# Six-bit weights read as float16 bit patterns, byte-paired words, and a rearranged start, in a fused conditioning and feed-forward kernel

## Chip, cores and metric

The kernel runs on one core of one Trainium2 chip. The metric is device time in microseconds (us). The time before is the median of three runs, 272.76 us (272.31 to 272.89).

## What is computed

The reference, cut to what matters:

```python
x: (64, 64, 1024) float32; itok: (64,) int32; weights: (16, 64, 64) float32
qweight: (1024, 768) int32; scale, zero_point: (1024, 1); bias: (1024,)
W = weights[itok]
h = einsum('bct,bcd->bdt', x, W)
p = qweight.reshape(1024, 256, 3)
v0, v1 = p[:, :, 0] & 63, p[:, :, 0] >> 6 & 63
v2, v3 = p[:, :, 1] & 63, p[:, :, 2] & 63
w = (stack([v0, v1, v2, v3], axis=2).reshape(1024, 1024) - zero_point) * scale
out = x + einsum('bsk,nk->bsn', h, w) + bias
```

Each of the 64 batches picks one of 16 small matrices, multiplies its 64 x 1024 block of x by it, and then multiplies the result by one shared 1024 x 1024 matrix of six-bit integers, with a zero point and a scale for each output feature.

## The kernel before

Batches go in pairs: 32 pairs, each 128 partitions (2 x 64 channels) by 1024 features, and two pairs make a group that shares one tile of x. The features are laid out by field, so that each 128-row tile of the weights (KT = 8 tiles) is one field of the packed words: tiles 0 and 1 are v0, 2 and 3 are v1, 4 and 5 are v2, 6 and 7 are v3.

Float32 factors are replaced by two float16 parts, a rounded high part and the remainder as a low part, so that TensorE can work in 16 bits. A pair goes through two products:

- The **first product** (`stage1`, L437) multiplies x by the selected conditioning matrix. Before it, a power of two for each batch is found from a sum of magnitudes (`magnitudes` on ScalarE L257, `bounds` on TensorE L261, `scales` on VectorE with `powers` L129 to L133). `split_1` (ScalarE, L281) writes the scaled high part, `split_2` (VectorE, L291) the low part, and four transfers on SyncE's queue (`stack_high` L303 and L304, `stack_low` L308 and L309) stack the parts in the tile `xa`. The conditioning table `tab` is split into parts in the same manner once (`weights_scaled` L189, `weights_high` L192, `weights_low` L195), and each pair's matrices are copied from it by two transfers (`select_pair`, L233).
- The **second product** (L461) multiplies the first one's result, again split into `hh` (ScalarE, L449) and `hl` (VectorE, L453), by the integer weights `qT`: 8 tiles x 2 parts x 2 banks of 512 columns, 32 products for each pair.
- VectorE then scales the sums by the batch's and the feature's scales (L502) and adds x (L507). ScalarE and GpSimd add the zero point's part (`zero_points` L495 and L497, which needs the feature sums, L326) and the bias (`add_bias`, L490) to x in place beforehand. Even pairs accumulate in one PSUM tile and odd pairs in another, so a pair's second product waits until the result of the pair two before has been read.

The order of instructions on every engine is written out by hand. A steady loop, `window(p)` from pair 3 on, issues the first product of pair p+1, the results of pair p-1, the splitting of a later group and then the second product of pair p.

Pairs 0 and 1 (group 0) have a start of their own, so that TensorE has real work early. Fifty products of a dummy (WARM, L520) come first. Their first products are done in float32 straight from x and the selected matrices (`early_stage1`, L383). Their scales come from a bound: the largest magnitude of x in each partition (`early_largest`, VectorE, L363) times the largest magnitude in each row of the selected matrix, which GpSimd copies from a table (`early_select`, L351 and L354); `early_rows` (L367) forms the product, `early_bounds` (TensorE, L371) sums it over the partitions, and `early_scales` turns it into powers of two. `early_high` (ScalarE, L391) and `early_low` (VectorE, L398) split the result. Pairs 0 to 3 have their results kept aside by `early_out` (L417, L421), which adds the zero point's part, and GpSimd adds these to x later (`early_add`, L426) in the windows named by `LATE` (L660).

In the same stretch the packed words arrive as six blocks of 16-bit halves (`load_q`, L76), VectorE masks or shifts out the six bits (`unpack`, L144 and L146), and a second instruction on VectorE or ScalarE (`centre`, L152 and L154) converts the integers to float16 less 32 (QMID). The zero points are turned into 32 less themselves (L600). The scale of the conditioning table is found by a float32 product with the identity (`weights_turn`, L170) and another that spreads the diagonal (`weights_bounds`, L182).

SyncE issues nearly all transfers, in program order.

Of the kernel before, what the change touches and what calls it, by code (L numbers as in the profile page):

```python
# [18 lines left out]
QMID = 32.0  # L19
# [9 lines left out]
def adaln_ffn(ctx: ExitStack, tc: tile.TileContext, x, cond, cw, qw, ws, wz, bias, out):  # L29
# [9 lines left out]
    WARM = 50  # L39
# [20 lines left out]
    def load_pair(p):  # L60
        g, i = divmod(p, 2)
        if i == 0:
            xts[g] = xp.tile([P, 2, T], F32, name="xt")
        nc.sync.dma_start(xts[g][:, i, :], xf[:, p, :])
# [6 lines left out]
    NW = qw.shape[1] // P  # L71
    qr = qp.tile([P, NW, N], U16, name="qr", bufs=1)
    qv = qw.rearrange("h (w p) n -> h p w n", p=P)

    def load_q(w, n=1):
        nc.sync.dma_start(qr[:, w : w + n, :], qv[0, :, w : w + n, :])  # L76
# [9 lines left out]
    load_pair(0)  # L86
    load_q(0)
    load_q(1)
    load_pair(1)
    load_q(2, 2)  # L90
    load_q(4, 2)
# [24 lines left out]
    spread = const.tile([NK, P], F32, name="spread")  # L116
# [7 lines left out]
    eye = const.tile([P, P], F32, name="eye")  # L124
    nc.vector.tensor_scalar(eye, off, 0, None, ALU.is_equal)

    def powers(sums, up, down):

        nc.vector.tensor_scalar(sums, sums, LEAST, None, ALU.max)  # L129
        nc.vector.tensor_scalar(  # L130
            down.bitcast(I32), sums.bitcast(I32), EXPONENT, EXPONENT, ALU.bitwise_and, ALU.bitwise_xor
        )
        nc.vector.tensor_scalar(up.bitcast(I32), sums.bitcast(I32), EXPONENT, None, ALU.bitwise_and)  # L133


    qT = const.tile([P, KT, N], F16, name="qT")
    qis = {}

    def unpack(kt, n=1):

        qi = qp.tile([P, n, N], U16, name="qi", tag=f"qi{n}")
        w = kt if kt < 2 else kt - 2
        if kt in (2, 3):
            nc.vector.tensor_scalar(qi, qr[:, w : w + n, :], 6, 63, ALU.logical_shift_right, ALU.bitwise_and)  # L144
        else:
            nc.vector.tensor_scalar(qi, qr[:, w : w + n, :], 63, None, ALU.bitwise_and)  # L146
        for m in range(n):
            qis[kt + m] = qi[:, m, :]

    def centre(kt, eng):  # L150
        if eng is nc.scalar:
            nc.scalar.activation(qT[:, kt, :], qis[kt], AF.Copy, bias=-QMID)  # L152
        else:
            eng.tensor_scalar(qT[:, kt, :], qis[kt], 1.0, -QMID, ALU.mult, ALU.add)  # L154
# [7 lines left out]
    wmx = const.tile([P, NK], F32, name="wmx")  # L162
# [10 lines left out]
    def weights_diagonal():  # L173
        most = const.tile([NK, 1], F32, name="most")
        nc.vector.tensor_reduce(most, tmp["pt"], AX.X, ALU.max)
        diag = const.tile([NK, NK], F32, name="diag")
# [20 lines left out]
    def weights_hot():  # L197

        hot = const.tile([NK, B], F32, name="hot")
# [5 lines left out]
        up_w = const.tile([NK, P], F32, name="up_w")  # L205
# [61 lines left out]
    def unscales(g):  # L267
        nc.vector.scalar_tensor_tensor(st[g]["u"], st[g]["up"], 0.25, wupb[:, 2 * g : 2 * g + 2], ALU.mult, ALU.mult)

    def scales_in_full(g):  # L270

        pl = st[g]["pl"]
        powers(pl, pl, st[g]["down"])
        nc.vector.scalar_tensor_tensor(st[g]["u"], pl, 0.25, wupb[:, 2 * g : 2 * g + 2], ALU.mult, ALU.mult)
# [36 lines left out]
    def split_sums(g):  # L311
        xs = st[g]["xs"]
        xh = sp.tile([P, 2, 2], F16, name="xh")
        for j, (h, o) in enumerate(((LO, HI), (HI, LO))):
            nc.scalar.copy(xh[h, :, j], xs[h, :])  # L315
            for i in range(2):
# [18 lines left out]
    def unscale_sums(g):  # L335
        for j, h in enumerate((LO, HI)):
            nc.vector.tensor_tensor(st[g]["hs"][h, :], st[g]["pu"][h, :, j], st[g]["u"][h, :], ALU.mult)  # L337


    xm = const.tile([P, 2], F32, name="xm")  # L340
    wm = const.tile([P, 2], F32, name="wm")
    pb = const.tile([P, 2, 2], BF, name="pb")
    updown = const.tile([P, 2, 2, 2], F32, name="updown")

    def early_select():

        for p in range(2):
            ks = []
            for j, h in enumerate((LO, HI)):
                k = nc.gpsimd.value_load(cb[0:1, 2 * p + j : 2 * p + j + 1], min_val=0, max_val=NK - 1)  # L350
                nc.gpsimd.tensor_copy(wbd[h, p, h], w32[h, ds(k, 1), :].rearrange("p o d -> p (o d)"))  # L351
                ks.append((h, k))
            for h, k in ks:
                nc.gpsimd.tensor_copy(wm[h, p : p + 1], wmx[h, ds(k, 1)])  # L354

    def early_sums(p):
        if 0 not in st:
            st[0] = {n: const.tile([P, 2], F32, name=n + "0") for n in ("xs", "u", "hs")}
# [3 lines left out]
    def early_largest(p):  # L362
        nc.vector.tensor_reduce(xm[:, p : p + 1], xts[0][:, p, :], AX.X, ALU.max, apply_absolute_value=True)  # L363

    def early_rows(p):

        nc.vector.tensor_scalar(pb[:, p, :], half, xm[:, p : p + 1], wm[:, p : p + 1], ALU.mult, ALU.mult)  # L367

    def early_bounds(p):
        pl = ps_s.tile([P, 2], F32, name="pl", tag="s")  # L370
        nc.tensor.matmul(pl, lhsT=all_ones, rhs=pb[:, p, :], start=True, stop=True)  # L371
        tmp["pl"] = pl

    def early_scales(p):
        powers(tmp["pl"], updown[:, p, 0, :], updown[:, p, 1, :])

    def early_unscales(p):
        for j, h in enumerate((LO, HI)):
            nc.vector.tensor_scalar(st[0]["u"][h, p : p + 1], updown[h, p, 0, j : j + 1], 0.5, None, ALU.mult)

    def early_stage1(p, ph, kts=range(KT)):
        for n, kt in enumerate(kts):
            nc.tensor.matmul(  # L383
                ph[:, n, :, :], lhsT=xts[0][:, p, ts(kt, P)], rhs=wbd[:, p, :], start=True, stop=True
# [29 lines left out]
    def early_out(p):  # L414
# [3 lines left out]
            pos[p], pos[p], st[g]["u"][:, i : i + 1], tmp["zt", p], ALU.mult, ALU.add  # L418
# [57 lines left out]
    def stage2_bank(p, n, ks=range(2)):  # L476
        if p not in pos:
            pos[p] = ps_o[p % 2].tile([P, N], F32, name="po", tag="po")
        for k in ks:
            products(pos[p], p, range(KT), [k], [BANKS[n]], [BANKS[n]])  # L480
# [11 lines left out]
    def zero_points(p):  # L492
# [4 lines left out]
        nc.gpsimd.tensor_tensor(xt, xt, zt, ALU.add)  # L497
# [28 lines left out]
    weights_largest()  # L526
    early_select()
    for n in range(2, 6):
        conditions_of(n)
    early_sums(0)  # L530
    early_largest(0)
    early_rows(0)
    early_stage1(0, ph0a, range(0, 4))
    early_bounds(0)
    unpack(0)
    early_scales(0)
    early_high(0, ph0a, LOWER)
    early_stage1(0, ph0b, range(4, KT))
    centre(0, nc.vector)
    unpack(1)  # L540
    centre(1, nc.vector)
    early_high(0, ph0b, UPPER)
    early_sums(1)
    stage2_tiles(0, range(0, 2), [0])
    early_low(0, ph0a, LOWER)
    early_stage1(1, ph1)
    unpack(2, 2)
    centre(2, nc.scalar)
    centre(3, nc.scalar)
    stage2_tiles(0, range(0, 2), [1])  # L550
    weights_turn()
    stage2_tiles(0, range(2, 3))
    early_largest(1)
    early_rows(1)
    unpack(4, 2)
    centre(4, nc.vector)
    early_bounds(1)
    stage2_tiles(0, range(3, 4))
    magnitudes(1, 0)
    centre(5, nc.scalar)  # L560
    early_low(0, ph0b, UPPER)
    early_scales(1)
    weights_diagonal()
# [3 lines left out]
    centre(6, nc.vector)  # L567
    early_high(1, ph1, slice(0, KT))
    stage2_tiles(0, range(5, 6))
    weights_bounds()  # L570
    scales(1, FIRST)
    centre(7, nc.vector)
    split_1(1, 0)
    stack_high(1, FIRST)
    load_x(3)
    magnitudes(1, 1)
    weights_powers()
    stage2_tiles(0, range(6, KT))
# [4 lines left out]
    bounds(1, SECOND)  # L583
    scales(1, SECOND)
    split_1(1, 1)
    weights_scaled()
    weights_high()
# [5 lines left out]
    select_pair(2)  # L593


    stage2_tiles(1, range(0, 4), [0])
    early_feature_sums(0)
    early_unscales(0)
    early_unscales(1)
    nc.scalar.activation(zsb, zsb, AF.Copy, bias=QMID, scale=-1.0)  # L600
    early_zero_points(0)
    stage2_tiles(1, range(0, 4), [1])
    stack_high(1, SECOND)
    split_2(1, 1)
    stack_low(1, SECOND)
    select_pair(3)
    nc.sync.dma_start(bib, bias.partition_broadcast(P))
    select_pair(4)
    select_pair(5)
    weights_hot()  # L610
    early_out(0)
    stage2_tiles(1, range(4, 7))
    magnitudes(2, 0)
    split_sums(1)
    ph = stage1(2)
    stage1_high(2, ph)
    magnitudes(2, 1)
    stage2_tiles(1, range(7, KT))
    early_feature_sums(1)
    early_zero_points(1)  # L620
# [3 lines left out]
    stage2_bank(2, 0, [0])  # L624
# [162 lines left out]
```

## Time and profile before

| | |
|---|---|
| median of three runs | 272.76 us |
| profiled execution | 272.38 us |
| its span, first to last instruction | 270.6 us |
| mean granted TensorE clock | 0.998 |
| TensorE products busy | 263.2 us (97% of the span) |
| VectorE busy | 204.8 us (76%) |
| ScalarE busy | 162.3 us (60%) |
| GpSimd busy | 168.2 us (62%) |
| second products (L461), hh and hl | 496 each of 512 columns, mean 379 ns |
| chain that ended last | TensorE 83% (L461 alone 70%), VectorE 10%, transfers 4% |

Times in the profile count from the start of the span. PE is TensorE, PEld its load of the stationary factor, DVE VectorE, ACT ScalarE, POOL GpSimd, SP SyncE; a q behind an engine's name means its queue of transfers. A group is written as output<-inputs, shapes, the number of instructions, its busy time, the mean of one in ns, and the idle time before it with what ended that. Products are pipelined, so a mean of 379 ns is a product's latency: the stream passes 32 of them in 6.91 us. The chain of waits is followed back from the last instruction, at each step to what released it.

Landings of the first loads, worked out from the issue times and times to landing: conditioning matrices 4.43 us, x of pair 0 5.82, the first two blocks of words 6.99 and 7.73, x of pair 1 9.01, the other words 10.4 and 11.7, x of pair 2 13.0 and of pair 3 15.3.

### The profile page before, as it was taken

To read this page: it belongs to the slowest core of one execution; us is meant where nothing else is said; L and a number is where in the kernel's file an instruction comes from. 1 tells how busy PE (TensorE), PEld (TensorE's weight loads), DVE (VectorE), ACT (ScalarE), POOL (GpSimd) and SP (SyncE) were. 2 spreads that over 40 slices of the span, in tenths; PEclk is the share of its full clock that TensorE was granted. 3 is DMA by queue.
4 is the path that set the end of the run, shared out by engine and by line. 5 is a ranking of instruction groups with operands and counts; after the bars stand their busy time and mean duration, and the time that the engine had idled before them with its cause. 6 is when DMAs were issued, how large, how long until landed. Compare 5 with 4: busy or idle time off the path is not lost.

```text
span 270.6 us, 5751 instructions
## 1 busy us (share of the span) xinstructions
PE 263.2 (97%) x2170; PEld 142.2 (53%) x2170; DVE 204.8 (76%) x272; ACT 162.3 (60%) x289; POOL 168.2 (62%) x87
## 2 busy tenths in 40 slices
PE   8999989999999999999999999999999999999994
PEld 8645545455555545555554555555455555545553
DVE  3989799795695959869595985959599595955543
ACT  3788897576565667656566765656676565634100
POOL 4100069969789595978959593874919387495200
PEclk9999999999999999999999999999999999999999
DMA  7997666975878796686965897696776765551203
GB/s 238 403 333 239 150 147 184 202 241 127 285 207 247 247 265 220 146 303 183 285 198 156 256 251 237 183 291 173 206 227 167 213 181 148 166 157 78 79 18 139
DMA packets 35836, 55.30 MB, mean 204 GB/s; under 512 B 18400, under 2 KB 18656, under 8 KB 35808
## 3 DMA queue, kind: packets, MB, share of 16 engines
q1 hardware_dynamic: 35776, 54.93, 68.1%
q8 instruction: 17, 0.28, 0.4%
q14 instruction: 11, 0.09, 0.1%
q10 hardware_dynamic: 32, 0.00, 0.0%
HBM read 20.45 MB, written 16.78 MB: 138 GB/s over the span
## 4 chain that ended last, share of the span: by engine, by line
PE 83%; DVE 10%; DMA 4%; ACT 1%; issue 1%; SPq 0%; DVEq 0%; ACTq 0%
PE po L461 70%; PE ph L437 9%; DVE lf L291 3%; PE pe L461 3%; DMA xa<-lf 2%; DMA xt<-in_x_dram 2%; DVE po L417 1%; DVE res L421 1%; DMA wst<-tab 1%; DVE hl L453 1%; PE ph L383 1%; PE pu L326 0%; ACT hf L281 0%; DVE xm L363 0%; DVE tab L195 0%
## 5 line engine op out<-in xcount | busy, mean ns | idle before, releaser
L461 PE MATMUL po<-qT,hh 128*128 128x512 f16 x496 | 118.5, 379 | 0.7 <-ACT hh L391 0.4
L461 PE MATMUL po<-qT,hl 128*128 128x512 f16 x496 | 118.5, 379 | 0.0
L497 POOL TENSOR_TENSOR xt<-xt,zt 128x1024 f32<-128x1024 f32 x28 | 79.3, 2852 | 51.4 <-ACT zt L495 51.4
L490 POOL TENSOR_TENSOR xt<-xt,bib 128x1024 f32<-128x1024 f32 x32 | 76.5, 2412 | 28.0 <-DVE hs L337 25.4
L461 PEld LDWEIGHTS <-hl 128*128 128x128 f16 x520 | 50.8, 98 | 59.1
L449 ACT CAST hh<-ph 128x1024 f16<-128x1024 f32 x30 | 30.3, 1011 | 80.9 <-PE ph L437 42.5
L461 PEld LDWEIGHTS <-hh 128*128 128x128 f16 x520 | 48.2, 98 | 52.7 <-ACT hh L391 0.6
L502 DVE SCALAR_TENSOR_TENSOR po<-po,u,scb 128x1024 f32<-128x1024 f32 x27 | 34.8, 1287 | 50.6 <-PE po L461 50.6
L291 DVE SCALAR_TENSOR_TENSOR lf<-xt,down,hf 128x1024 f16<-128x1024 f32 x30 | 62.4, 2118 | 0.7 <-ACT hf L281 0.7
L437 PEld LDWEIGHTS <-xa 128*128 128x128 f16 x960 | 32.3, 98 | 9.1 <-issue 1.5
L453 DVE TENSOR_TENSOR hl<-ph,hh 128x1024 f16<-128x1024 f32 x30 | 36.5, 1216 | 0.0
L281 ACT ACTIVATE hf<-xt,down 128x1024 f16<-128x1024 f32 x30 | 34.2, 1144 | 2.4 <-DVE down L130 2.2
L437 PE MATMUL ph<-wst,xa 128*128 128x64 f16 x960 | 33.3, 193 | 1.7 <-DMA xa<-lf 0.8
L507 DVE TENSOR_TENSOR xt<-po,xt 128x1024 f32<-128x1024 f32 x27 | 33.1, 1225 | 2.2 <-DVE po L502 0.5
L257 ACT ACTIVATE junk<-xt 128x1024 bf16<-128x1024 f32 x30 | 31.7, 1056 | 1.0 <-DMA xt<-in_x_dram 0.3
L495 ACT ACTIVATE zt<-zsc,hs 128x1024 f32<-128x1024 f32 x28 | 30.5, 1137 | 0.0
L318 ACT ACTIVATE xh<-xh,xs 64x1 f16<-64x1 f16 x60 | 14.4, 287 | 1.0
L426 POOL TENSOR_TENSOR xt<-xt,res 128x1024 f32<-128x1024 f32 x4 | 9.4, 2359 | 0.0
L461 PE MATMUL pe<-qT,hh 128*128 128x256 f16 (+1 forms) x24 | 6.6, 308 | 0.0
L520 PE MATMUL pc<-dummy 128*128 128x128 bf16 x50 | 5.5, 311 | 1.1 <-DVE one L102 1.1
L461 PE MATMUL pe<-qT,hl 128*128 128x256 f16 (+1 forms) x24 | 6.5, 308 | 0.0
L315 ACT CAST xh<-xs 64x2 f16<-64x2 f32 x30 | 5.7, 191 | 0.2
(82 smaller groups left out, 108.4 us busy)
## 6 DMA issues: line engine op xcount, KB each, us to landing
out_dram<-xt SPq DMA_DIRECT2D x31, 512.0 KB, 3.0
xt<-in_x_dram SPq DMA_DIRECT2D x14, 1024.0 KB, 7.6
xa<-hf SPq DMA_DIRECT2D x26, 256.0 KB, 3.8
xa<-lf SPq DMA_DIRECT2D x26, 256.0 KB, 3.8
xt<-in_x_dram SPq DMA_DIRECT2D x4, 512.0 KB, 7.6
wst<-tab SPq DMA_DIRECT2D x60, 32.0 KB, 3.0
qr<-in_L_ffn_qweight_dram SPq DMA_DIRECT2D x2, 512.0 KB, 7.6
xa<-hf SPq DMA_DIRECT2D x8, 128.0 KB, 3.0
```

The lines of the kernel that those rows point to most:

```text
L257: nc.scalar.activation(junk, xts[g][:, i, :], AF.Abs, accum_out=st[g]["l1"][:, i : i + 1])
L281: nc.scalar.activation(st[g]["hf"][:, i, ts_], xts[g][:, i, ts_], AF.Copy, scale=st[g]["down"][:, i : i + 1], accum_out=st[g]["xs"][:, i : ...
L291: nc.vector.scalar_tensor_tensor(st[g]["lf"][:, i, ts_], xts[g][:, i, ts_], st[g]["down"][:, i : i + 1], st[g]["hf"][:, i, ts_], ALU.mult, ...
L437: nc.tensor.matmul(ph[:, kt, j, :], lhsT=st[g]["xa"][:, i, j, ts(kt, P)], rhs=wsts[g][:, i, a, j, :], start=(a == 0), stop=(a == 1),)
L449: nc.scalar.copy(hs_pair[p][0][:, kts, :], ph[:, kts, :])
L453: nc.vector.tensor_tensor(hl[:, kts, :], ph[:, kts, :], hh[:, kts, :], ALU.subtract)
L461: nc.tensor.matmul(po[:, a], lhsT=hs_pair[p][k][:, kt, :], rhs=qT[:, kt, c], start=(kt == 0 and k == 0), stop=(kt == KT - 1 and k == 1),)
L490: nc.gpsimd.tensor_tensor(xt, xt, bib, ALU.add)
L495: nc.scalar.activation(zt, zsc, AF.Copy, scale=st[g]["hs"][:, i : i + 1])
L497: nc.gpsimd.tensor_tensor(xt, xt, zt, ALU.add)
L502: nc.vector.scalar_tensor_tensor(po, po, st[g]["u"][:, i : i + 1], scb[:, cols], ALU.mult, ALU.mult)
L507: nc.vector.tensor_tensor(xts[g][:, i, cols], po, xts[g][:, i, cols], ALU.add)
```

## The change

- **Weights.** The unpacked six bits are written straight into the tile that the second products read; its 16-bit words are taken as float16 bit patterns, so that an integer v stands for v x 2^-24 (QUNIT). `centre`, its tile and the pass over the zero points go. The factor 2^-24 is put into the scales (`0.25 / QUNIT`, `0.5 / QUNIT`, `unscale_sums`), and the zero point's part is subtracted instead of added.
- **Packed words.** The host's layout puts the six-bit bytes in pairs: four blocks instead of six; tiles 2 and 3 are blocks 0 and 1 shifted by 6, tiles 6 and 7 are blocks 2 and 3 shifted by 8.
- **Loads.** Pair 0's x comes in two halves; pair 1's x comes ahead of the words.
- **Bounds of pairs 0 and 1.** GpSimd copies only the selected matrices, and VectorE takes their largest magnitude (`early_weights`). For pair 0's first half of features and for pair 1, ScalarE's sum of magnitudes takes the place of the largest; pair 0's second half stays on VectorE. The clamp moves from `powers` into `early_rows`.
- **Order.** Both pairs' float32 first products come ahead of any second product. The small products of the conditioning scales use bfloat16 and move forward, as does the table. The sums of x for pairs 0 and 1 move back. WARM is 43.
- **Rest.** Group 1's `xh` remainders are subtracted on GpSimd. Pair 2's first six tiles are queued ahead of `bounds(2)`. The bias of pairs 0 and 1 moves from ahead of the loop into the windows, with the early adds.

The diff, cut to its core:

```diff
-    WARM = 50
+    WARM = 43
-    nc.sync.dma_start(xts[g][:, i, :], xf[:, p, :])
+    nc.sync.dma_start(xts[g][:, i, ts_], xf[:, p, ts_])
-    load_pair(0)
+    load_pair(0, slice(0, T // 2))
+    load_pair(0, slice(T // 2, T))
+    load_pair(1)
     load_q(0)
     load_q(1)
-    load_pair(1)
     load_q(2, 2)
-    load_q(4, 2)
-    spread = const.tile([NK, P], F32, name="spread")
+    spread = const.tile([NK, P], BF, name="spread")
-    eye = const.tile([P, P], F32, name="eye")
+    eye = const.tile([P, P], BF, name="eye")
-    qT = const.tile([P, KT, N], F16, name="qT")
+    q16 = const.tile([P, KT, N], U16, name="q16")
+    qT = q16.bitcast(F16)
...
-        if kt in (2, 3):
-            nc.vector.tensor_scalar(qi, qr[:, w : w + n, :], 6, 63, ALU.logical_shift_right, ALU.bitwise_and)
+        w = kt if kt < 2 else kt - 2 if kt < 6 else kt - 4
+        to, of_ = q16[:, kt : kt + n, :], qr[:, w : w + n, :]
+        if kt in (2, 3, 6, 7):
+            nc.vector.tensor_scalar(to, of_, 6 if kt < 4 else 8, 63, ALU.logical_shift_right, ALU.bitwise_and)
...
-    def centre(kt, eng):
-        if eng is nc.scalar:
-            nc.scalar.activation(qT[:, kt, :], qis[kt], AF.Copy, bias=-QMID)
-        else:
-            eng.tensor_scalar(qT[:, kt, :], qis[kt], 1.0, -QMID, ALU.mult, ALU.add)
...
-        nc.vector.scalar_tensor_tensor(st[g]["u"], st[g]["up"], 0.25, wupb[...], ALU.mult, ALU.mult)
+        nc.vector.scalar_tensor_tensor(st[g]["u"], st[g]["up"], 0.25 / QUNIT, wupb[...], ALU.mult, ALU.mult)
...
+            if g == 1:
+                nc.gpsimd.tensor_tensor(xh[o, :, j], xs[h, :], xh[h, :, j], ALU.subtract)
+                continue
...
-                nc.gpsimd.tensor_copy(wm[h, p : p + 1], wmx[h, ds(k, 1)])
+    def early_weights(p):
+        wl = const.tile([P, 1], F32, name=f"wl{p}")
+        nc.vector.tensor_reduce(wl, wbd[:, p, :], AX.X, ALU.max, apply_absolute_value=True)
+        nc.vector.tensor_scalar(wm[:, p, :], half, wl[:, 0:1], None, ALU.mult)
...
+    def early_magnitudes(p, n, ts_, eng):
+        if eng is nc.scalar:
+            nc.scalar.activation(junk[:, ts_], xts[0][:, p, ts_], AF.Abs, accum_out=xm[p, n])
+        else:
+            nc.vector.tensor_reduce(xm[p, n], xts[0][:, p, ts_], AX.X, ALU.max, apply_absolute_value=True)
...
+    def early_rows(p, n):
+        nc.vector.tensor_scalar(pb[:, p, n, :], wm[:, p, :], xm[p, n][:, 0:1], LEAST, ALU.mult, ALU.max)
...
-    LATE = {5: (early_add, 0), 7: (early_add, 1), 9: (add_bias, 2), 11: (early_add, 2), 13: (add_bias, 3), 15: (early_add, 3)}
+    LATE = {5 + 2 * n: ((add_bias, early_add)[n % 2], n // 2) for n in range(8)}
```

The start after the change, in the order written (selections and transfers of later pairs left out):

```python
    early_select(0)
    early_select(1)
    weights_largest()
    early_weights(0)
    early_magnitudes(0, 0, HALF[0], nc.scalar)
    early_stage1(0, ph0a, range(0, 4))
    early_rows(0, 0)
    early_magnitudes(0, 1, HALF[1], nc.vector)
    early_rows(0, 1)
    early_stage1(0, ph0b, range(4, 6))
    early_bounds(0, 2)
    early_stage1(0, ph0b, range(6, KT))
    early_scales(0)
    early_high(0, ph0a, LOWER)
    early_high(0, ph0b, UPPER)
    unpack(0)
    early_stage1(1, ph1)
    weights_turn()
    early_weights(1)
    unpack(1)
    early_low(0, ph0a, LOWER)
    stage2_tiles(0, range(0, 2), [0])
    weights_diagonal()
    early_low(0, ph0b, UPPER)
    early_magnitudes(1, 0, ALL, nc.scalar)
    weights_bounds()
    stage2_tiles(0, range(0, 2), [1])
    early_sums(0)
    unpack(2, 2)
    weights_powers()
    early_rows(1, 0)
    stage2_tiles(0, range(2, 3))
    early_bounds(1, 1)
    early_scales(1)
    stage2_tiles(0, range(3, 4))
    magnitudes(1, 0)
    early_high(1, ph1, slice(0, KT))
    unpack(4, 2)
    weights_scaled()
    stage2_tiles(0, range(4, 5))
    bounds(1, FIRST)
    unpack(6, 2)
    scales(1, FIRST)
    weights_high()
    stage2_tiles(0, range(5, KT))
    early_low(1, ph1, slice(0, KT))
    split_1(1, 0)
    stack_high(1, FIRST)
    split_2(1, 0)
    stack_low(1, FIRST)
    weights_low()
```

## The prediction

> **What bounds the kernel now.** I read the chain of waits first, in order of time, then the busy time by stretch, then the timeline of the first 60 us. By stretch (engine columns are busy us with instruction counts):
>
> ```profile
> core 0: us, PE busy (x) PEld busy (x) DVE busy (x) ACT busy (x) POOL busy (x), PEclk, DMA share, GB/s
> ...
> 55.00:250.00 195.00, 195.00 (x1632) 101.55 (x1629) 149.18 (x173) 119.90 (x215) 143.65 (x58) 1.00 0.71 208
> ```
>
> From 55 us on TensorE never stops, at full clock, and the edits there take nothing off its queue. So the change can only move the moment at which this unbroken stretch begins. In the chain (start, us, what) I look for pieces that are not TensorE, and for TensorE work that is not a product:
>
> ```profile
> 5.82 1.23 DVE xm L363
> ...
> 8.23 0.85 ACT hh L391 x2
> 9.08 0.05 issue
> 9.13 1.04 PE po L461 x4
> 10.17 1.78 PE ph L383 x16
> 11.95 0.86 PE po L461 x4
> 12.81 0.32 PE pt L170 x2
> ...
> 16.75 0.32 PE pw L182 x2
> ...
> 23.05 2.35 DMA wst<-tab
> ...
> 49.10 4.94 DMA xa<-lf
> 54.05 0.14 issue
> 54.18 1.04 PE ph L437 x30
> ```
>
> The last wait on the path is at 54.18: the first products of pair 6 wait for a transfer of low parts. Everything behind it is TensorE to the end. The timeline shows what was late before it (idle time and releaser in brackets):
>
> ```profile
> 25.74 1.19 PE L437 MATMUL ph<-wst,xa 128*128 128x64 f16 x32 [0.43 <-DMA wst<-tab]
> ...
> 28.13 1.89 PE L461 MATMUL po<-qT,hh 128*128 128x512 f16 x8 [0.22 <-DVE hs L406]
> ...
> 29.64 2.88 SPq L233 DMA_DIRECT2D wst<-tab  x4
> ...
> 37.79 1.03 PE L437 MATMUL ph<-wst,xa 128*128 128x64 f16 x30 [0.40 <-DMA xa<-lf]
> ...
> 38.46 8.90 POOL L490 TENSOR_TENSOR xt<-xt,bib 128x1024 f32<-128x1024 f32 x3 [2.54 <-DVE lf L291]
> ...
> 43.86 4.58 DVE L291 SCALAR_TENSOR_TENSOR lf<-xt,down,hf 128x1024 f16<-128x1024 f32 x2
> ```
>
> So the start is a relay of small waits, about 3 us of TensorE idle between 9 and 54 us. I follow TensorE's queue through it and set my time for each point beside that of before. A product of 512 columns takes 0.216 us of the stream (6.91 us for 32).
>
> **Up to the first scales.** The conditioning weights land at 4.43 in both. VectorE then has, in order: largest weights 1.22 (L166), the reduce of the selected weights (new, 128 elements; near row: L175, 0.27), their row (near row: L177, 0.22), the bounds of x's first half (L367, 0.29), the reduce of x's second half, its bounds (0.29), and about 0.03 between dependants. For the half reduce (512 elements) no row stands: half of L363's 1.22 is 0.61, all of it 1.22. The Trainium skill, "VectorE: DVE Perf Modes", section on the TRN2 errata, gives (N+151)/0.96 for a one-per-cycle float32 add, which gives 1.22 at 1024 as measured, and 0.69 here; I take 0.69, as an estimate. Sum: 4.43+1.22+0.27+0.22+0.29+0.69+0.29+0.1 = 7.5, against 7.52 before. Halving pair 0's magnitude work thus buys nothing by itself: the weights' chain took its place. The clamp L129 (0.17) leaves the path; the high parts start at 8.0 instead of 8.23.
>
> The halves of x: "DMA: Bandwidth & Descriptors" of the skill, section on the anatomy of one DMA, gives each transfer (there on GpSimd's path) a fixed cost of about 2 us on top of its bytes and so speaks against cutting 512 KB in two (2 us more on the first scales if paid in line). But here the two 256 KB word loads, issued back to back, land 0.74 us apart (6.99 and 7.73), and 512 KB loads 1.3 to 1.4 us apart: the fixed part is overlapped in the queue. I take 5.15 and 5.85 for the halves (whole: 5.82), pair 1's x at 7.4 (9.01), words at 8.2 and 8.8 (6.99, 7.73), the rest from 10.2 on. All of that meets its reader except that the first word load is about 0.1 late for VectorE. Half a megabyte fewer words also brings everything behind forward by 1.3 us (x of pair 3 15.3 to about 13.5), hidden.
>
> **TensorE, step by step.** Seven warm-up products fewer at 105 ns (5.25 us for 50) free it at 5.6 instead of 6.3; the granted clock reads 1.00 in each stretch of the first 9 us, and the longest new gap behind the warm-up is 0.4 us, so I give the shorter warm-up no price. A float32 first product takes 0.244 (16 half-records in 1.95 us). Six of pair 0 run 5.65 to 7.1, then it waits for the bounds (7.5), and ten more (two of pair 0, eight of pair 1) take 2.44: 10.1. The turn of the weights in bf16 costs 0.1 instead of 0.32. The first second product starts at 10.2, which is 1.1 later than before, but the 1.78 of pair 1's first products and the 0.32 lie behind it.
> - Field tiles 0 and 1, both halves: 8 x 0.216 = 1.73, plus 0.1 for the bf16 bounds of the weights: 12.05. Tile 2 needs its words: VectorE has low parts to 10.2, the diagonal (0.27+0.22) to 10.8, low parts 0.87 to 11.65, the unpack 0.69 to 12.35. It starts at 12.4 (13.07). Five 0.42 us conversions on VectorE and three of 1.04 on ScalarE have gone; without that no reordering would fit here.
> - Tiles 2 to 7: 24 x 0.216 = 5.2, two bounds and 0.15 of waiting for the unpack of tile 4: 17.9 (18.95, where a float32 step of 0.32 lay inside). Pair 1's low parts, which must be finished before its bank is written, end at 17.7 (18.89).
> - Pair 1, tiles 0 to 6: 28 x 0.216 = 6.06, feature sum 0.3: 24.3. The selected weights: low parts to 18.95, table low 1.22 to 20.1, transfers issued 20.2 and 20.9, landing 2.0 to 2.6 later: 23.5. The 0.6 of waiting before 25.74 goes; start 24.3 (25.74).
> - First product of pair 2 (0.93), tile 7, sum: 26.4 (28.13). Pair 0's result must have left its bank; that ends at 25.6 (27.99).
> - Bank 0 of pair 2: 3.46; bounds; the bf16 product of the batches' scales 0.1 instead of a gap of 0.46: first product of pair 3 at 30.2 (32.15).
> - 0.93 and 3.46: 34.6. Pair 4's low parts: VectorE ends them at 30.6 (33.04), SyncE is through its four weight issues (2.88) at 29.5 and the two high parts at 30.7, issues the low ones to 31.9, landing 2.3 later: 34.2. Start 34.7 (37.79). This has 0.5 us in hand.
> - The feature sums of group 2 then wait some 0.35 for ScalarE's small copies (16 us of unbroken ScalarE queue before it). Then 0.93+0.1+6.91+0.93+6.93: the first product of pair 6 at 51.0.
> - Its transfer: before, the low parts of group 3 took 4.58 because four GpSimd additions ran alongside; undisturbed they take 2.47 (at 58.46). Two of the four (pairs 0 and 1) move to windows 5 and 9. Low parts end at about 44, land at 48 or 49 even at 4.94 us: no wait (before 0.65).
>
> Gain: 54.18 - 51.0 = 3.2 us. The moved additions: GpSimd has one extra operation of 2.4 per two windows, up to window 19 instead of 15; windows with one show 12.87 of 16.00 busy and TensorE 16.00, so they cost nothing; without that cover the low parts would take 4.58 for 2.47, and that still meets a deadline a window away. Stores of pairs 0 to 3 go later by one to two windows, off the path. Subtract for add and the other scale factor: same instructions. GpSimd's two xh differences (near row: copies at 0.23) replace four ScalarE steps of 0.26 and are read 2 us later.
>
> Profiled execution: 272.38 around a span of 270.6; 3.2 less is 269.2. The median of before is 0.38 above that execution: 269.6.
>
> **Rivals.**
> A. *The cover is too thin.* The 0.3 to 0.5 us in hand at the unpack of tile 2, at pair 2's bank and at SyncE's queue (where one high-part issue took 1.35 instead of 0.6) is used up, so only the front part, up to pair 3 (1.95), and perhaps the 0.65 at the end stay: 272.76 - 2.0 = 270.8. For it: five dependants within 0.5 us. Against: SyncE's and VectorE's queues move forward with TensorE's.
> B. *Nothing waits.* From 10.2, 160 products 34.6, four first products 3.7, small ones 0.9: 49.4, and 0.3 to 0.8 of waits: 268.4.
> C. *Slower: the bit patterns.* Integers 0 to 63 as float16 bits are all below the smallest normal value. If TensorE streamed such columns slower, each of the 1,040 second products would pay; the gain is eaten at 3.2/1040 = 3 ns each, and 5 ns would give 274.8. Against: hh and hl products both average 379 ns although the low parts are some 2,000 times smaller; no row shows such a moving operand.
> D. *The first second product, 1.1 us later, is never caught up*: pair 1's high parts or the words bind instead: 272.8.
>
> **The numbers.** Forecast (268.9 to 270.2) 0.58; A 0.20; B 0.12; D 0.04; C 0.06. The range 268.3 to 271.6 takes in A and B and leaves out C, D and the ends. 0.2% is about what a measurement here can tell from no change. Faster 0.89 (forecast, A, B less a little), same 0.05, slower 0.06.
>
> **What would show it.** First second product near 10.2 and later than before; tile 2 near 12.4; no wait of the first products of pair 2 for wst nor of pair 6 for xa; low parts of group 3 near 2.5 us for two; 0.38 us products unchanged. Wrong if TensorE's unbroken stretch starts at 52.5 or later, if the halves of x land more than 1.3 us apart, or if the mean of a second product rises.

## The result, and the profile after

The changed kernel takes 272.54 us (median of 12 executions, 271.86 to 273.49); the kernel before 272.5 us (12 executions, 272.3 to 273.0). The ratio is 0.9999, with an interval of 0.9986 to 1.0012: no change that can be measured, where 3.2 us were forecast. The profiled execution of the changed kernel took 271.98 us around a span of 270.2.

Start of each step on TensorE, in us (the last column is the ninth experiment below, in which only two loads stand elsewhere):

| step | before | forecast | after | two loads moved |
|---|---|---|---|---|
| first second product | 9.13 | 10.2 | 10.21 | 10.80 |
| field tile 2 of pair 0 | 13.07 | 12.4 | 12.54 | 13.00 |
| second product of pair 1 | 18.95 | 17.9 | 17.99 | 18.46 |
| first product of pair 2 | 25.74 | 24.3 | 24.20 | 24.66 |
| second product of pair 2 | 28.13 | 26.4 | 26.40 | 26.86 |
| first product of pair 3 | 32.15 | 30.2 | **32.40** | 30.69 |
| first product of pair 4, main part | 37.79 | 34.7 | **37.99** | 35.56 |
| first product of pair 6, main part | 54.18 | 51.0 | **53.73** | 52.16 |
| unbroken from there to the end | yes | yes | yes | yes |

Down to pair 2 the forecast holds within 0.15 us. Between 26.40 and 32.40 the whole lead is lost. The stretch from 55 us on is TensorE without a break, as before:

```profile
core 0: us, PE busy (x) PEld busy (x) DVE busy (x) ACT busy (x) POOL busy (x), PEclk, DMA share, GB/s
55.00:250.00 195.00, 195.00 (x1621) 101.44 (x1620) 151.29 (x173) 119.79 (x215) 146.61 (x59) 1.00 0.69 206
```

The chain of waits now runs through a piece that it did not have before (start, us, what):

```profile
22.02 7.27 DMA xt<-in_x_dram
29.28 0.02 issue
29.30 0.63 SPq L227
...
34.19 3.67 DMA xa<-lf
37.85 0.14 issue
37.99 1.03 PE ph L442 x30
```

A 1 MB load of x is issued at 22.02 and lands at 29.29, and 0.01 us later SyncE goes on, at 29.30, with the transfers of pair 4's weights. The low parts of pair 4, the last of which SyncE issues at 34.19, are then what pair 4 waits for. The timeline shows the same stretch from TensorE's and SyncE's side (idle time and releaser in brackets):

```profile
25.29 1.46 SPq L227 DMA_DIRECT2D wst<-tab  x2
...
26.80 0.61 SPq L610 DMA_DIRECT2D bib<-in_L_ffn_bias_dram  x1
29.30 2.88 SPq L227 DMA_DIRECT2D wst<-tab  x4
...
32.27 0.19 PE L323 MATMUL pu<-xh,wst 128*128 128x2 f16 x2 [1.96 <-DMA wst<-tab]
32.40 1.16 PE L442 MATMUL ph<-wst,xa 128*128 128x64 f16 x32
```

The weights of pair 3, 32 KB each, were issued from 25.29 on and landed 6.0 to 6.7 us behind their issue; before, those of pairs 2 and 3 took 1.9 to 2.6. The profile gives it for the two transfers of pair 3 after, and for the four of pairs 2 and 3 before:

```profile
DMA to landing us min/median/max: 6.0/6.3/6.7
DMA to landing us min/median/max: 1.9/2.0/2.6
```

The feature sums need them and stand ahead of pair 3's first product, so TensorE is idle for 1.96 us there.

The load is the x of pairs 6 and 7. In the kernel before it stands between the high and the low parts of pair 2: issued at 18.89, it landed by 24.8. The change moved it behind the weights of pair 2. SyncE's queue in the timeline, first before, then after:

```profile
18.26 0.59 SPq L304 DMA_DIRECT2D xa<-hf  x1
18.89 0.59 SPq L68 DMA_DIRECT2D xt<-in_x_dram  x1
21.75 0.46 SPq L308 DMA_DIRECT2D xa<-lf  x1
...
27.40 1.45 SPq L233 DMA_DIRECT2D wst<-tab  x2
```

```profile
20.50 1.48 SPq L227 DMA_DIRECT2D wst<-tab  x2
22.02 0.61 SPq L69 DMA_DIRECT2D xt<-in_x_dram  x1
22.73 0.50 SPq L297 DMA_DIRECT2D xa<-hf  x1
```

What the transfers did meanwhile (two stretches before, then the same two after):

```profile
core 0: us, PE busy (x) PEld busy (x) DVE busy (x) ACT busy (x) POOL busy (x), PEclk, DMA share, GB/s
16.80:24.80 8.00, 7.95 (x40) 3.84 (x41) 7.48 (x18) 6.86 (x10) 0.00 (x0) 1.00 0.87 282
24.80:31.20 6.40, 5.75 (x57) 3.33 (x56) 5.25 (x15) 5.57 (x13) 0.00 (x0) 1.00 0.64 144
...
16.80:24.80 8.00, 8.00 (x59) 4.02 (x57) 6.67 (x13) 6.53 (x11) 0.00 (x0) 1.00 0.58 123
24.80:31.20 6.40, 5.39 (x43) 2.72 (x39) 5.38 (x17) 5.14 (x9) 0.39 (x2) 1.00 1.06 291
```

The stretch in which the load used to travel has become the emptier one (share 0.58, before 0.87), and in the next one the transfer engines are busy throughout (1.06, before 0.64). Share and GB/s go apart: from 19.2 to 21.6 us, when only the parts and weights of pair 2 travel, the share is 0.89 to 0.96 at 195 to 210 GB/s, so GB/s alone would have shown more room than there was.

### The profile page after: what moved, and what is told of

The parts are those of the page before. It is cut to its first block, busy times and chain, and to the rows that moved or that the text cites. A ratio compares the mean times of both kernels' runs of the same rounds, so it can differ in the third digit from the quotient of the medians.

```text
span 270.2 us, 5723 instructions
## 1 busy us (share of the span) xinstructions
PE 261.1 (97%) x2161; PEld 140.0 (52%) x2161; DVE 201.4 (75%) x269; ACT 159.3 (59%) x285; POOL 166.2 (61%) x85
## 4 chain that ended last, share of the span: by engine, by line
PE 85%; DMA 6%; DVE 4%; SPq 3%; issue 1%
PE po L466 72%; PE ph L442 10%; DMA xt<-in_x_dram 3%; PE pe L466 3%; DMA qr<-in_L_ffn_qweight_dram 2%; DMA xa<-lf 1%; SPq L227 1%; DVE hl L403 1%; PE pu L323 1%; DVE q L148 1%; DVE lf L285 0%; SPq L65 0%; DVE q L146 0%; DVE wsc L183 0%; DVE tab L189 0%
## 5 line engine op out<-in xcount | busy, mean ns | idle before, releaser
L466 PE MATMUL po<-q,hh 128*128 128x512 f16 x496 | 118.5, 379 | 0.4 <-DVE q L146 0.2
L466 PE MATMUL po<-q,hl 128*128 128x512 f16 x496 | 118.5, 379 | 0.0
L495 POOL TENSOR_TENSOR xt<-xt,bib 128x1024 f32<-128x1024 f32 x32 | 75.4, 2379 | 7.5 <-DMA wst<-tab 5.5
L507 DVE SCALAR_TENSOR_TENSOR po<-po,u,scb 128x1024 f32<-128x1024 f32 x27 | 34.7, 1287 | 50.7 <-PE po L466 50.7
L315 ACT ACTIVATE xh<-xh,xs 64x1 f16<-64x1 f16 x56 | 13.4, 287 | 0.9
L466 PE MATMUL pe<-q,hh 128*128 128x256 f16 (+1 forms) x24 | 6.6, 308 | 0.0
L466 PE MATMUL pe<-q,hl 128*128 128x256 f16 (+1 forms) x24 | 6.5, 308 | 0.0
L334 DVE SCALAR_TENSOR_TENSOR hs<-pu,u 64x2 f32<-64x2 f32 x30 | 4.6, 153 | 1.7 <-PE pu L323 1.6
```

Of the source, the lines that this page charges most:

```text
L466: nc.tensor.matmul(po[:, a], lhsT=hs_pair[p][k][:, kt, :], rhs=qT[:, kt, c], start=(kt == 0 and k == 0), stop=(kt == KT - 1 and k == 1),)
L495: nc.gpsimd.tensor_tensor(xt, xt, bib, ALU.add)
L507: nc.vector.scalar_tensor_tensor(po, po, st[g]["u"][:, i : i + 1], scb[:, cols], ALU.mult, ALU.mult)
```

## The experiments

Theory Q: what failed is the place of this one load. Transfers issued behind it land 6 to 7 us behind their issue, and SyncE's eighth issue behind it waits until it has landed (in these traces SyncE's transfers signal their landing on eight semaphores in turn). Rival I: the lead would have gone anyway, because other work was the next late thing. From the fifth run on, rival R: the transfers as a whole are short of capacity, and a new place only moves the wait.

**1. The load among the first loads.**

```diff
     load_x(2)
+    load_x(3)
...
     magnitudes(1, 1)
-    load_x(3)
```

> The changed kernel with the load of group 3's x (1 MB) issued with the first loads, behind that of group 2, instead of behind the selected weights of pair 2. Theory Q (the load, moved in SyncE's queue to 22.02 us, took 7.3 us; pair 3's parts and weights lay behind it in the transfer queue, and SyncE's eighth next issue waited for it): TensorE's wait of 2.0 us for pair 3's weights at 32.24 and most of the wait before pair 4's first product go, that product starts near 35 instead of 37.99, time 269.3 to 270.3. Rival I (SyncE's queue is bound by the number of its issues, some 28 of 0.6 to 0.7 us between 18 and 35 us, and pair 4's low parts leave at about 34 us whatever stands where; both kernels do start pair 4 near 37.9): pair 4's first product stays later than 37, time 271.8 to 272.6.

Measured: 270.74 us (270.27 to 271.21), ratio to before 0.9936 (0.9922 to 0.9949); pair 3 at 31.28, pair 4 at 36.08. Rival I falls: 1.7 us of the gain come back by moving one load. It is 0.4 us above the end of what Q expected, because the load now lies ahead of pair 2's weights. From the chain of waits of this kernel:

```profile
20.91 4.19 DMA wst<-tab
25.10 0.04 issue
25.14 1.22 PE ph L443 x32
```

The load was issued at 9.1 and landed at 23.7: it stood last in a line of loads that ran at about 410 GB/s without a pause until 19 us; pair 2's weights, issued from 20.91 on, landed at 25.10 and cost TensorE 0.37 us. The eighth issue behind this load, a high part of pair 3, went out at 23.68, when it had landed.

**2. The load where it was before**, between the high and the low parts of pair 2.

```diff
     stack_high(1, FIRST)
+    load_x(3)
     split_2(1, 0)
...
     magnitudes(1, 1)
-    load_x(3)
```

> The changed kernel with the load of group 3's x at its old place in SyncE's queue, between the high and the low parts of pair 2 (issue near 19 us). Theory Q: the load is through by about 25 us, nothing of pair 3 is behind it, but pair 2's low parts and weights now are, so the wait in front of pair 2's first product may come back (0.3 to 1.5 us); time 269.8 to 271.2. Rival I: 271.8 to 272.6.

Measured: 273.42 us (272.25 to 274.14), ratio 1.0041 (1.0026 to 1.0055); the profiled execution took 272.25 at full clock, and four of the seven had a mean granted clock of 0.990 to 0.994 (see the last section). Q's number is missed with and without these four. Its mechanism is there, one pair further forward (timeline of TensorE):

```profile
26.98 1.28 PE L442 MATMUL ph<-wst,xa 128*128 128x64 f16 x32 [2.03 <-DMA wst<-tab]
```

In the old order of the work SyncE could issue pair 2's low parts only at 21.75, well behind the load at 18.89, and the weights at 23.05; in the new order the low parts are ready at once, so the load at 19.66 has the low parts at 20.34 and pair 2's weights at 21.64 close behind it, and these land 5.30 us later. So it is not the move alone that was wrong: in the new order of the work the old place doesn't fit either.

**3. Only the move, in the kernel before.**

```diff
     stack_high(1, FIRST)
-    load_x(3)
...
     select_pair(2)
+    load_x(3)
```

> The kernel before with nothing changed but the load of group 3's x put behind the selected weights of pair 2, where the changed kernel has it. Theory Q: it lands near 31.5 us, pair 3's parts and weights behind it, SyncE's eighth next issue waits; pair 3's first product (32.15) and pair 4's (37.79) each start 1 to 2.5 us later: 273.7 to 275.0. Rival I: the same issues in another order, 272.5 within 0.4.

Measured: 275.55 us (275.43 to 275.74), ratio 1.0115 (1.010 to 1.013): 3.1 us for one line. TensorE waits 2.30 us for pair 3's weights and 0.94 for the low parts of pair 6. SyncE stops as in the changed kernel (its queue in the timeline):

```profile
24.60 0.61 SPq L68 DMA_DIRECT2D xt<-in_x_dram  x1
...
31.93 2.88 SPq L233 DMA_DIRECT2D wst<-tab  x4
```

The load takes 7.3 us, so it lands at 31.9; the eighth issue behind it starts at 31.93. In the kernel before, the move by itself costs about what was forecast for the whole change.

**4. The bias additions of pairs 0 and 1 early again**, on top of run 1: the two go back ahead of the loop, and the windows' table of late additions is the one of the kernel before.

```diff
     add_bias(5)
+    add_bias(0)
+    add_bias(1)
-    LATE = {5 + 2 * n: ((add_bias, early_add)[n % 2], n // 2) for n in range(8)}
+    LATE = {5: (early_add, 0), 7: (early_add, 1), 9: (add_bias, 2), 11: (early_add, 2), 13: (add_bias, 3), 15: (early_add, 3)}
```

> e1 with the bias of pairs 0 and 1 added ahead of the loop, as in the kernel before, and with its table of late work. Theory of the prediction: four GpSimd additions beside VectorE's low parts of group 3 make these take 4.58 instead of 2.47 us for two, and the first product of pair 6 then waits for their transfer, some 0.3 to 0.7 us: e1 plus 0.5. Rival: that wait came from how late TensorE's deadline stood to SyncE's queue; with the front earlier it is as late as before or later. If GpSimd's additions do not matter: e1 within 0.2.

Measured: 273.5 us (271.84 to 275.35, 22 executions), 2.8 above run 1; the profiled spans differ by 1.7. In the profile, the two low parts of group 3 take 6.62 us beside GpSimd's additions, SyncE issues them at 49.55, and pair 6 starts at 54.27 after 0.96 and 0.89 us of waiting. A cost of 0.5 was expected: the moved additions are worth 1.7 us of the span once TensorE is early enough to need them. The rest of the 2.8 is another effect: in 12 of the 22 executions the mean granted clock was 0.990 to 0.994. The other ten have a median of 272.4, which is 1.6 above run 1 and agrees with the spans. Why the clock falls in this version is open: the profiled execution kept it, and its longest idle gap of TensorE is 0.96 us.

**5. The load further on, behind pair 3's weights**, and the bias behind those of pair 5.

```diff
     magnitudes(1, 1)
-    load_x(3)
...
     select_pair(3)
-    nc.sync.dma_start(bib, bias.partition_broadcast(P))
+    load_x(3)
     select_pair(4)
     select_pair(5)
+    nc.sync.dma_start(bib, bias.partition_broadcast(P))
```

> The changed kernel, with the 1 MB load of the x of pairs 6 and 7 moved on in SyncE's program from behind the weights of pair 2 to behind those of pair 3, and the load of the bias from there to behind the weights of pair 5. Theory Q (what failed is the place of this load: the transfers issued behind it land 7 us later, and SyncE's eighth issue behind it waits until it has landed): now only the weights of pairs 4 and 5 stand close behind it, and they are read 8 us later. First product of pair 3 without a wait at 30.2 to 30.9, of pair 4 at 35.0 to 35.8, of pair 6 at 51.2 to 52.0; 269.5 to 270.5 us. Rival R (the transfers as a whole are short of capacity up to 30 us, and a new place only moves the wait): pair 3 or 4 waits for another transfer, or ScalarE's magnitudes of pairs 6 and 7 come too late; 271.3 to 272.8 us.

Measured: 273.94 us (271.79 to 275.66, 22 executions), ratio 1.0054 (1.0035 to 1.0073). Pair 3 starts at 30.43 without a wait, as Q has it and as forecast. But then (timeline of TensorE):

```profile
37.96 0.23 PE L442 MATMUL ph<-wst,xa 128*128 128x64 f16 x2 [2.99 <-DMA xa<-lf]
...
39.66 3.20 PE L466 MATMUL po<-q,hh 128*128 128x512 f16 x8
42.70 1.89 PE L466 MATMUL po<-q,hl 128*128 128x512 f16 x8
```

The low parts of pair 4, the last issued at 33.22, now lie behind the load and the bias, land 5.02 us later, and TensorE waits 2.99 us. R is right for this version, though the median lies above its range too. The eight products behind that wait take 3.20 us instead of 1.89: the granted clock was 0.50 from 38.94 us on, for 3.41 us. With the columns as in the first fence (the clock is the third figure from the end), the profile has:

```profile
38.94:42.35 3.41, 3.41 (x28) 1.74 (x25) 3.26 (x10) 2.62 (x4) 3.15 (x2) 0.50 0.94 319
```

**6. The load in ScalarE's queue.**

```diff
-    def load_x(g):
+    def load_x(g, eng=nc.sync):
...
-        nc.sync.dma_start(xts[g], xf[:, 2 * g : 2 * g + 2, :])
+        eng.dma_start(xts[g], xf[:, 2 * g : 2 * g + 2, :])
...
     magnitudes(1, 1)
-    load_x(3)
...
     split_1(1, 1)
+    load_x(3, nc.scalar)
```

> The changed kernel, with the same 1 MB load issued by ScalarE in its own queue, at about the same time (behind the high parts of pair 3, at some 22.0 us), everything else in its place. If it is SyncE's own queue and its order (theory Q) that made the transfers behind the load late: the weights of pair 3 land 2 to 3.5 us behind their issue, SyncE does not stop at 26.8 us, first product of pair 3 at 30.2 to 31.0, of pair 4 at 35.0 to 36.0; 269.6 to 270.8 us. If it is the 16 engines that all queues share (rival R): the transfers issued at 22.7 to 25.3 still land 5 to 7 us later, first product of pair 3 at 32 or later; 271.5 to 272.8 us, though even then SyncE's stop at 26.8 to 29.3 may be gone.

Measured: 273.38 us (271.82 to 274.93), ratio 1.0039 (1.0022 to 1.0056). ScalarE came to the issue at 21.32, earlier than meant and just ahead of pair 2's second transfer of weights, which shows the matter all the better. From the chain:

```profile
21.81 5.66 DMA wst<-tab
```

These 32 KB stand in SyncE's queue with no load ahead of them there, and still land 5.66 us later. So the delay is not the order within one queue: the engines that carry both queues are what is shared, and R is right on that. SyncE's stop shrinks to 0.5 us (26.98 to 27.48): it reaches pair 4's weights at 27.96 (29.30 in the changed kernel). TensorE waits 2.63 us for these weights of pair 2, and pair 3 starts at 34.85. The median lies above R's range: the 12 executions with a mean clock of 0.997 or more have a median of 272.8, and the other eight, at 0.991 or 0.994, took 273.5 to 274.9.

**7 and 8. Run 5 with 50 warm-up products; run 5 with pair 0's x in one transfer.**

```diff
-    WARM = 43
+    WARM = 50
```

> As the run with the load behind pair 3's weights, with 50 warm-up products of TensorE instead of 43. The prediction gave the shorter warm-up no price: then the seven products of 105 ns (0.7 us) only delay the first products, of which some is caught up at the wait for the unpack of field tile 2; 0.0 to 0.6 us above that run. Rival: the shorter warm-up costs clock or leaves TensorE cold, and 50 is at least 0.4 us faster than that run.

```diff
-    load_pair(0, slice(0, T // 2))
-    load_pair(0, slice(T // 2, T))
+    load_pair(0)
```

> As the run with the load behind pair 3's weights, with the x of pair 0 loaded in one transfer of 512 KB instead of two of 256 KB (its magnitudes are still taken in halves). The prediction said that halving buys nothing by itself, since the chain of the weights ends later than the x: within 0.3 us of that run. Rival: the early first half is what lets the first six first products go ahead of the scales, and without it the front end is 0.4 to 0.8 us later; or two transfers cost more than one, and whole is faster by over 0.3 us.

Measured: 273.83 us (273.57 to 275.12) and 273.96 us (271.63 to 275.15), beside 273.94 for run 5. Neither median moves, and in both runs nearly all executions have the lower clock of run 5 (six of six and five of six), so that little can be told from the times. The profiles tell more. With 50 products the first second product starts at 10.68 (run 5: 10.44) and field tile 2 at 12.74 (12.75): the shorter warm-up shows no price and hardly a gain. With x whole, field tile 2 starts at 12.01, 0.74 earlier. Over all profiles with the halves (nine, 50 products included) it starts between 12.54 and 13.13, with the whole (three) at 12.01, 12.23 and 12.29.

**9. Run 5 with the bias last**, behind the last low parts of group 2.

```diff
     select_pair(5)
-    nc.sync.dma_start(bib, bias.partition_broadcast(P))
...
     stack_low(2, SECOND)
+    nc.sync.dma_start(bib, bias.partition_broadcast(P))
```

> As the run with the load behind pair 3's weights, with the 512 KB load of the bias moved on from behind the weights of pair 5 to behind the last low parts of group 2 (some 36 us). In that run pair 3 started without a wait at 30.43, but pair 4 waited 3.0 us for low parts that landed 5.0 us behind their issue, close behind the bias. Theory Q (a transfer lands late by what stands ahead of it in SyncE's queue): now the low parts of pair 4 land 2.3 to 3.3 us behind their issue, pair 4 starts at 34.9 to 35.6, pair 6 at 51.0 to 52.2; 269.0 to 270.4 us, and no long gap of TensorE, so no execution with a clock below 0.996. Rival R (the wait only moves again, to the additions of the bias by GpSimd, which now run beside the low parts of group 3, or to pair 6): 271.3 us or more.

Measured: 270.21 us (269.61 to 270.89), ratio 0.9926 (0.9906 to 0.9946), no execution with a clock below 0.997. Q holds: pairs 3 and 4 start at 30.69 and 35.56. What is left can be read in VectorE's and TensorE's timeline:

```profile
35.56 1.23 PE L442 MATMUL ph<-wst,xa 128*128 128x64 f16 x32 [0.32 <-DVE hl L458]
...
42.43 4.59 DVE L285 SCALAR_TENSOR_TENSOR lf<-xt,down,hf 128x1024 f16<-128x1024 f32 x2
...
52.16 1.03 PE L442 MATMUL ph<-wst,xa 128*128 128x64 f16 x30 [0.37 <-DMA xa<-lf]
```

With the bias late, GpSimd's additions fall beside the low parts of group 3 again (4.59 us instead of 2.47), and a little of the old wait of pair 6 is back. This version is faster than both kernels.

**10 and 11. Runs 9 and 1 with pair 0's x whole** (the edit of run 8).

> As the run with the bias last, with the x of pair 0 in one transfer of 512 KB. Theory H (the second half costs SyncE one more issue of some 0.45 us ahead of the words, whose first load ends the front's chain): first second product 0.3 to 0.6 us earlier, and the whole 0.3 to 0.7 us below the run with the bias last: 268.5 to 270.0 us. Rival (as the prediction had it, halving changes nothing): within 0.2 us of it.

> As the first run (the load of pairs 6 and 7 among the first loads; 270.74 us), with the x of pair 0 in one transfer. Theory H: 270.0 to 270.5 us. Rival (halving changes nothing, or the queue of loads, which is full until 23 us, sets the time here anyway): 270.6 to 270.9 us.

Measured: 270.21 us (269.11 to 270.51; ratio 0.9915, 0.9895 to 0.9934) beside 270.21 for run 9, and 270.56 us (269.65 to 271.09; ratio 0.9945, 0.9928 to 0.9962) beside 270.74 for run 1. Theory H is right on the front and its total isn't seen: in run 10 the first second product starts at 10.21 (10.80), pair 3 at 29.98 and pair 4 at 34.85, but pair 6 then waits 1.09 us for its low parts (0.37) and starts at 52.26 (52.16). Between runs 11 and 1 the medians differ by 0.2 us, within their spread.

**12. Run 5 with its gap filled**: 45 products that nothing reads, ahead of pair 4's first product.

```diff
+        if p == 3:
+            pf = ps_s.tile([P, P], F32, name="pf", tag="s")
+            for _ in range(45):
+                nc.tensor.matmul(pf, lhsT=dummy, rhs=dummy, start=True, stop=True)
```

> As the run with the load behind pair 3's weights (which waits 3.0 us ahead of pair 4 and had 5 executions at 271.8 to 272.4 us with a mean clock of 0.997 or more, and 17 at 273.4 to 275.7 us with 0.986 to 0.994), with 45 small products of no use (128 columns, nothing reads them; some 2.5 us at full clock) in that gap, ahead of the first product of pair 4. Theory G (the idle gap of TensorE is what takes its clock down, and the lower clock costs the 1.3 to 3 us behind it): all executions at 271.6 to 272.6 us, clock 0.996 or more. Rival (the clock falls for another reason, such as the way the work is spread over the engines): the same two groups as before, median 273.6 to 274.1 us.

Measured: 272.41 us (271.84 to 273.48), all 22 executions with a mean clock of 0.997 or more, where run 5 had 17 of 22 at 0.986 to 0.994. In the timeline of TensorE the 45 products run from 34.84 to 37.5; then:

```profile
38.06 1.33 PE L442 MATMUL ph<-wst,xa 128*128 128x64 f16 x32 [0.54 <-DMA xa<-lf]
...
39.35 1.89 PE L466 MATMUL po<-q,hh 128*128 128x512 f16 x8
```

Pair 4 starts as late as in run 5, and the products behind it are at full speed. Theory G holds for the clock: with the gap filled it no longer falls, and that is 1.5 us of run 5's median. Not all times are in its range of 271.6 to 272.6: four executions took 273.2 to 273.5 us at full clock, and what made them longer is open.

## Why the prediction was wrong

**The step that failed** is "SyncE is through its four weight issues (2.88) at 29.5" together with "first product of pair 3 at 30.2". SyncE was through at 32.18 and pair 3 started at 32.40. The prediction took the times to landing of the trace of before (2.0 to 2.6 us for the weights, 2.3 for low parts) for a queue whose order the change alters: `load_x(3)` moves from ahead of pair 2's low parts to behind pair 2's weights. Neither the list of changes nor the sums contain this line. By the trace of before it had a price: the load took 5.9 us to land there, and pair 3's weights, issued 3.3 us behind it in the new order, are read at 30.1. Run 3 prices the move alone at 3.1 us in the kernel before. That this equals the forecast gain is partly chance: in the new order a better place brings back 1.7 (run 1) to 2.0 us (run 9), and the old place brings nothing (run 2). Run 9 moves the bias too; no run moves the bias alone.

**The size of the rest.** With the load and the bias placed so that nothing waits long for them (run 9), the ratio of 0.9926 stands for 2.0 us (1.5 to 2.6) of the 3.2 forecast. Its profile accounts for the difference at pair 6, 52.16 against 51.0: 0.5 that is there at pair 3 already (0.6 at field tile 2, where the words come late), 0.32 for the wait for VectorE's `hl` at pair 4, and 0.37 for pair 6's low parts.

**Point by point.**
- *Up to the first scales*: right in the number, 7.52 (forecast 7.5), in part by luck. The half reduce took 0.67 us, where 0.69 was estimated from the Trainium skill ("VectorE: DVE Perf Modes", section on the TRN2 errata) against 0.61 or 1.22 from the rows. But the weights landed 0.3 us earlier than forecast, and VectorE then waited 0.53 us for ScalarE's sum over x's first half, which the sum of the prediction left out. So x's first half set this time, and not the weights' chain:

```profile
6.36 0.31 DVE L371 TENSOR_SCALAR pb<-wm,xm 128x2 bf16<-128x2 f32 x1 [0.53 <-ACT junk L366]
```

- *Landing of the halves*: wrong, without harm to TensorE's times in the changed kernel's profile. The first half lands at 5.60 in the changed kernel, and the whole 512 KB at 5.44 (run 8) to 5.71 (run 10): cutting the load brought the first half no earlier. The two halves landed more than the doubted 1.3 us apart in run 9, where TensorE waits for the second until 7.23. The extra issue, some 0.45 us of SyncE, also puts the words behind it later: they land at 8.65 instead of the forecast 8.2, and VectorE waits 0.67 us for them instead of 0.1.
- *TensorE from 10.2 to 26.4*: right within 0.15 us, and with it the removal of `centre`, the bf16 steps, and the float32 first products ahead.
- *No wait of pair 2 for its weights*: right.
- *The moved bias additions*: right and under-rated. The two low parts of group 3 took 2.47 us and pair 6 had no wait; but run 4 shows 1.7 us of span for it where the forecast's share was 0.65.
- *The feature sums' wait of 0.35 us*: did not appear; at 38.89 they follow without idle time.
- *Warm-up without a price*: right (run 7), though it ended at 4.96 instead of 5.6, and TensorE then waited 0.75 us for x's first half instead of at most 0.4.
- *Rival C, the bit patterns*: fell. (Its count is off: 32 pairs of 32 products are 1,024, not 1,040; nothing rests on that.) The means of the second products of both parts are still 379 ns:

```profile
L466 PE MATMUL po<-q,hh 128*128 128x512 f16 x496 | 118.5, 379 | 0.4 <-DVE q L146 0.2
L466 PE MATMUL po<-q,hl 128*128 128x512 f16 x496 | 118.5, 379 | 0.0
```

- *Rival A, the cover is too thin*, named SyncE's queue as one of three places with 0.3 to 0.5 us in hand. The place was right; but the cause was 1 MB moved into the line, not the small stretch of issues that A thought of, and so its price was nearly three times that of A (3.2 us against 1.2).
- *Rival D, the late first second product never caught up*, has the right time for the wrong reason: it was caught up at 12.54.

What a reader could have seen beforehand: in the order of SyncE's queue the load changes place, and a load of 1 MB is the largest thing in that queue. The trace of before also shows what a large load does to what follows: the weights of pairs 4 and 5, issued there right behind the 512 KB of the bias, landed 3.6 to 4.8 us behind their issue.

## What to carry to other kernels

When a change reorders a queue of transfers, write down the new order with bytes, and give every small transfer behind a large one the landing time that the large one allows; times to landing from the trace of before belong to the order of before. Look for the stretch in which the DMA share is low, and put the large load where nothing behind it is due soon, which need not be as early as possible: in runs 1, 2 and 5 the load, or the bias, was still in the way of somebody, and in run 9 of hardly anybody. A load that is moved is a part of the change like any other, and a gain that was made step by step over 20 us can be lost at one such place.

## What the runs showed of the hardware

- **A 1 MB load holds up what is issued behind it, in whichever queue.** 32 KB transfers that land 1.9 to 2.6 us behind their issue took 3.5 to 6.7 us behind the load in SyncE's queue (runs 1 and 2, the changed kernel), and 5.66 when the load was in ScalarE's queue (run 6).
- **The eighth issue behind a load waits for its landing.** 29.30 against a landing at 29.29 in the changed kernel, 31.93 against 31.9 in run 3, 23.68 against 23.7 in run 1. With the load in ScalarE's queue SyncE stopped for 0.5 us only.
- **An idle gap of TensorE of 2.6 to 3.1 us can lower its clock.** In the profiles of runs 5, 6 and 7, with gaps of 2.99, 2.63 and 3.13 us, the granted clock is 0.50 for 3.41 us, beginning within 1 us of the gap's end; in that of run 8, with a gap of 2.99 us as in run 5, it stays at 1.00. Over all executions (their gaps aren't recorded) the lower mean clock came in 17 of 22 of run 5, 8 of 20 of run 6, and none of 22 with the gap filled (run 12). The Trainium skill ("TensorE: Matmul & The Clock Gate", section "HAM oscillation — how this bites in real kernels") warns of idle gaps above about 3.4 us, behind which products run at half the clock; here shorter ones were enough. Run 5's times lie in groups near 272.0, 273.9 and 275.4 us. The steps between them, 1.5 to 1.9 us, fit one or two such stretches (3.41 us at half the clock lose 1.7 us, an estimate from the profile). Runs 2, 3 and 4 and the changed kernel had some executions at 0.990 to 0.994 too, with gaps of 2.03, 2.30, 0.96 and 1.96 us in their profiles, which all kept the clock; what lowered it there is not shown. In the changed kernel these were 3 of 12 executions; without them its median would be 272.3, so this doesn't explain why the gain went missing.
- **The start varies.** With the same instructions up to 18 us, field tile 2 started at 12.54 in the profile of the changed kernel and at 13.13 in that of run 2, following the landing of the first loads: 0.6 us of the front are not a property of the kernel.
